# A cross-attention kernel on one core: value and output weights by quads of heads, and other tile shapes

## The chip, the cores and the metric

The kernel runs on one core of a Trainium2 chip. A core has a matrix engine (PE, TensorE), a vector engine (DVE), a scalar engine (ACT), a general engine (POOL, GpSimd), a queue engine (SP) that issues the DMAs here, an on-chip memory of 128 partitions (SBUF), and a matrix-result memory of 8 banks (PSUM), from which ACT and DVE copy results out.

The metric is the device time of one execution in microseconds. Before the change it was 272.81 us (median of three runs, 272.65 to 273.47). The profiled execution took 273.54 us.

## The reference, cut to what matters

Sixteen images of 256 tokens (width 256) attend to sixteen texts of 77 keys (width 192), with 8 heads of 256 each; then an output projection, a residual and a layer norm. All is float32.

```python
Q = (x @ Wq)        # Wq: 256 x (8*256)
K = (c @ Wk)        # Wk: 192 x (8*256)
V = (c @ Wv)        # Wv: 192 x (8*256)
score = einsum('bhqd,bhkd->bhqk', Q, K) / sqrt(256)      # masked by atten_mask
attn = softmax(score)
ctx = einsum('bhqk,bhkd->bqhd', attn, V)
out = ctx @ Wo + x                                       # Wo: (8*256) x 256
return (out - mean) * rsqrt(var + 1e-05) * gamma + beta
```

## The kernel before, in words

The kernel folds weights first. For each head h it forms G_h = Wk_h Wq_h^T (192 x 256) and U_h = Wv_h Wo_h (192 x 256). Scores of an image are then x (G_h^T c^T), and the output is the sum over heads of attn_h (c U_h). The 192 rows of the text width are split in 128 (held in `gA`, `uA`, contracted with `cA`) and 64 (held in `gB`, `uB`, contracted with `cB`); the 64-row parts of two heads or halves lie one above the other.

The order of work is written out by hand (`manual_schedule`): each engine runs its instructions in program order. PSUM tiles come from one pool, `ps_mm`, of 8 buffers, each a bank, all under the tag "mm" and taken in rotation: a new tile waits until the tile eight places earlier has been read out.

Before the main loop over images:

- SP issues all loads in order (lines 620 to 654): whole rows of Wk and Wq for the first head pair (`wk_nat`, `wq_nat`), the first texts, then for pairs a = 1 to 3 blocks `wk_blk` and `wq_blk` (four DMAs each, one for every 32 partitions), `wvT` (16 DMAs, pieces of 512 bytes), `wo_of` (four DMAs of 512 KB), the first images transposed by blocks (`xT`), the mask (`bias`) and the rest of the texts. A load waits for the one eight loads earlier.
- PE begins with `keep_busy(7)`, seven matmuls whose result is not used (L661). The first pair's G is made from transposes on PE (`turn_k`, `turn_q`, `g_of`).
- For pairs a = 1 to 3, DVE turns 32x32 blocks (`turn_blk`, L700), PE makes the 128 rows of G (`g_of_pair`, L798, 64x128 tiles) and the 64 rows (`rest_of_g_of_pair`, L814, 64x64 tiles); ACT copies the one to `gA`, DVE the other to `gB` (four copies, L823). Then `prepare_a` makes A = G^T c^T for the first four images, `part_A` from `gA` (L181, 128x32 tiles) and `part_B` from `gB` (L193, 64x32 tiles). For pair 1 the order is G, rest, A, B; for pairs 2 and 3 both B parts come at the end.
- DVE turns Wv (`turn_v`, L728, four calls, read with a step of 4 floats). PE then makes U: `of_pair` (L738, 64x128 tiles) gives the 128 rows in two halves j of two pairs each, every half in two banks of its own (`pu`); `rest_of_pairs` (L752, 64x64 tiles) gives the 64 rows, again in two halves (`pw`). ACT and DVE copy the results to `uA` (L878) and `uB` (L896). POOL adds up a fifth part of each (`sum_of`, L885 and L886).
- PE makes the scores of the first image (`scores`, L290, four banks). DVE turns the rest of the texts (`turn_rest`, L614 and L616; POOL copies parts of them to `cRA`, `cB`, `cRB`), then reads the score banks (`shift`, L307, 16 calls). ACT makes the exponentials.
- `prepare_last` treats the last 13 keys of all texts at once: eight banks `pr`, each 128 rows by two halves e; `part_A` (L249, 128x64 tiles, two to a bank) and `part_B` (L261, 64x64 tiles) in the order A(0), B(0), B(1), A(1). Four of its eight banks are those that held the scores.

Then the loop over images runs to the end: products with the texts (`pv`, `pa`), scores, softmax, the product with the values by seven block products in place of eight, layer norm, stores.

Of the kernel before, what the change touches and what calls it, by code (L numbers as in the profile page):

```python
# [27 lines left out]
def kernel(  # L28
# [212 lines left out]
    def prepare_last():  # L241


        pr = [ps_mm.tile([P, 2, B, KR], F32, tag="mm", name=f"pr_{n}") for n in range(DI // BK)]

        def part_A(e):
            for n, o in enumerate(pr):
                for i in range(2):
                    nc.tensor.matmul(  # L249
                        o[half(i), e].rearrange("p b k -> p (b k)"),  # L250
                        flat(of_e(uA, e)[:, n])[:, half(i)],
                        flat(cRA),
                        start=(e == 0),
                        stop=(e == 1),
                    )

        def part_B(e):
            for n in range(0, len(pr), 2):
                for i in range(2):
                    for k in range(2):  # L260
                        nc.tensor.matmul(  # L261
                            pr[n + k][half(i), e].rearrange("p b k -> p (b k)"),
                            flat(of_e(uB, e)[half(k), n + k])[:, half(i)],
                            flat(cRB[half(k)]),
                            start=(e == 1),
                            stop=(e == 0),
                        )

        part_A(0)
        part_B(0)  # L270
        part_B(1)
        part_A(1)
        for n, o in enumerate(pr):
            to = vr[:, :, n * BK : n * BK + 2 * KR]
            evacuate(to.rearrange("p b (e k) -> p e b k", e=2), o)
# [303 lines left out]
    with tc.tile_pool(name="wonce", bufs=1) as wp:  # L579
# [52 lines left out]
        wvT = wp.tile([P, NF, NL, P], F32, tag="wvT", name="wvT")  # L632
# [3 lines left out]
        wv_blocks = wv.rearrange("(m r) (a i f) -> a i r m f", r=BK, a=NF, i=NM)  # L636
        wo_rows = wo.rearrange("(a p n) f -> a p n f", p=P, n=4)
        for a in range(NF):
            load_blocks(wvT[:, a], wv_blocks[a])
        for a in range(NF):  # L640
            nc.sync.dma_start(wo_of[a // 2][:, a % 2], wo_rows[a])
# [21 lines left out]
        keep_busy(7)  # L663
# [61 lines left out]
        wv_turned = const.tile([P, NF, 4, DL], F32, tag="vr", name="wv_turned")  # L725

        def turn_v(a):
            nc.vector.transpose(  # L728
                wv_turned[:, a].rearrange("p n (m r) -> p m n r", r=BK),
                wvT[:, a].rearrange("p m (c n) -> p m n c", n=4),  # L730
            )


        def of_pair(out, a, weight, moving):

            for n in range(4):
                for e in range(2):
                    nc.tensor.matmul(  # L738
                        out[e][:, a % 2, :],
                        weight(a, e, n)[:, :P],  # L740
                        moving(a, e, n),
                        start=(n == 0),
                        stop=(n == 3),
                    )

        def rest_of_pairs(j, pairs, weight, moving, name):

            banks = [ps_mm.tile([P, DI], F32, tag="mm", name=f"{name}_{j}_{e}") for e in range(2)]
            for n in range(4):
                for i, a in enumerate(pairs):  # L750
                    for e in range(2):
                        nc.tensor.matmul(  # L752
                            banks[e][half(i)],
                            weight(a, e, n)[:, P:],
                            moving(a, e, n),
                            start=(n == 0),
                            stop=(n == 3),
                        )
            return banks

        def two_banks(name, j):
            return [ps_mm.tile([P, 2, DI], F32, tag="mm", name=f"{name}_{j}_{e}") for e in range(2)]

        def wv_part(a, e, n):
            return wv_turned[half(e), a, n]

        def wo_part(a, e, n):
            return wo_of[a // 2][half(e), a % 2, n, :]
# [24 lines left out]
        def g_of_pair(a):  # L793

            banks = [ps_mm.tile([P, DI], F32, tag="mm", name=f"pgb_{a}_{e}") for e in range(2)]
            for n in range(4):
                for e in range(2):
                    nc.tensor.matmul(  # L798
                        banks[e],
                        kT_blk[a][half(e), n, :P],  # L800
                        qT_blk[a][half(e), n],
                        start=(n == 0),
                        stop=(n == 3),
                    )
# [22 lines left out]
        def a_of_pairs(*pairs):  # L827
            part_A, part_B, copies = prepare_a(0, pairs)
            part_A()
            part_B()  # L830
            for dst, src in copies():
                nc.scalar.copy(dst, src)
# [11 lines left out]
        for a in range(1, NF):  # L844
            g_of_pair(a)
            if a == 2:
                turn_blk(3)
            rest_of_g_of_pair(a)
            if a == 1:
                turn_blk(2)  # L850
                a_of_pairs(1)
            if a == 2:
                second = prepare_a(0, (2,))
                second[0]()
        for i in range(3):
            turn_v(i)
        third = prepare_a(0, (3,))
        third[0]()
        for _, part_B, _ in (second, third):
            part_B()  # L860
        for _, _, copies in (second, third):
            for dst, src in copies():
                nc.scalar.copy(dst, src)
# [4 lines left out]

        for j in range(NF // 2):
            pu = two_banks("pu", j)  # L870
            for a in range(2 * j, 2 * j + 2):
                of_pair(pu, a, wv_part, wo_part)
            if j:
                for i in range(0, GT // 2, 2):
                    transpose_x(0, i)
                bias_of(0, GB)
            for e, copy in enumerate((nc.scalar.copy, nc.scalar.copy if j else nc.vector.tensor_copy)):
                copy(  # L878
                    of_e(uA, e)[:, :, 2 * j : 2 * j + 2].rearrange("p n a c -> p a n c"),
                    pu[e].rearrange("p a (n c) -> p a n c", c=BK),  # L880
                )
# [5 lines left out]

        sum_of(uA)
        for j in range(NF // 2):
            for e, pw in enumerate(  # L890
                rest_of_pairs(j, (2 * j, 2 * j + 1), wv_part, wo_part, "pw")
            ):
                copy = (nc.scalar.copy, nc.vector.tensor_copy)[e]
                for i in range(2):
                    for k in range(2):
                        copy(  # L896
                            of_e(uB, e)[half(k), :, 2 * j + i],
                            pw[half(i)].rearrange("p (n c) -> p n c", c=BK),
                        )
# [191 lines left out]
```

## Time and profile before

| | before |
|---|---|
| median of three runs | 272.81 us (272.65 to 273.47) |
| the profiled execution | 273.54 us |
| its span, first to last instruction | 271.6 us |
| PE busy | 265.3 us, 98% |
| PE weight loads busy | 192.1 us, 71% |
| DVE busy | 185.6 us, 68% |
| POOL busy | 171.4 us, 63% |
| ACT busy | 155.6 us, 57% |
| mean granted PE clock | 0.995 |

A line of a timeline gives the start and the length in us of equal instructions that follow each other, the engine, the line of the kernel, the operation, the tile written and the tiles read, the shape, and how many they are; in brackets stands the idle time before and what ended it. The chain is the work that ended last, followed back from the last instruction: start, length, engine, tile, line. Matmuls overlap, and their ends are modelled, so starts are the firmer numbers. A float32 matmul of the program stands in the trace as two.

### The profile page before, as it was taken

The numbers are of one execution on the slowest core, as the hardware profiler recorded it, in microseconds if no ns is written. First come the engines' busy times: TensorE is split into PE (matmuls) and PEld (weight loads), VectorE is DVE, ScalarE is ACT, GpSimd is POOL, SyncE is SP. The second block draws the span as 40 slices with busy tenths as digits, with TensorE's granted clock in tenths as the row PEclk, the third lists the DMA queues.
The fourth block names the chain that finished last, engine by engine and source line by source line (L and its number), as shares of the span: only waits on it lengthen the run. The fifth ranks groups of instructions, "written<-read, shape, count | busy, mean of one in ns | idle before, by whom it ended". The sixth has DMA issues, their size and how long they took to land.

```text
span 271.6 us, 14367 instructions
## 1 busy us (share of the span) xinstructions
PE 265.3 (98%) x6106; PEld 192.1 (71%) x6106; DVE 185.6 (68%) x809; ACT 155.6 (57%) x652; POOL 171.4 (63%) x231
## 2 busy tenths in 40 slices
PE   8999999999999999999999999999999999999993
PEld 8556588754894499549954996489769969694662
DVE  1455749584366757963795479646977798988765
ACT  3222415834758646873777386739584592945652
POOL 1000005724579766997599759964999798965654
PEclk9999999999999999999999999999999999999998
DMA  6999999998000010271018100910081010110102
GB/s 193 197 197 192 314 164 143 285 151 157 2 5 5 2 42 5 54 146 43 2 37 165 41 6 2 195 42 6 7 190 49 2 45 4 43 41 2 62 22 81
DMA packets 42512, 22.69 MB, mean 84 GB/s; under 512 B 23680, under 2 KB 41680, under 8 KB 42448
## 3 DMA queue, kind: packets, MB, share of 16 engines
q1 hardware_dynamic: 42448, 21.77, 36.8%
q8 instruction: 48, 0.79, 1.3%
q14 instruction: 16, 0.13, 0.2%
HBM read 17.57 MB, written 4.19 MB: 80 GB/s over the span
## 4 chain that ended last, share of the span: by engine, by line
PE 91%; DMA 5%; SPq 2%; DVE 1%; issue 0%; DVEq 0%
PE ps L290 25%; PE pa L181 11%; PE pv L215 10%; PE po L435 10%; PE pm L435 8%; PE pv L226 6%; PE pa L193 5%; DMA wk_blk<-in_L_xattn_Wk_dram 5%; PE po L368 4%; PE pu L738 3%; PE pr L249 2%; PE pgb L798 1%; PE pw L752 1%; PE pr L261 1%; SPq L597 1%; PE po L384 1%
## 5 line engine op out<-in xcount | busy, mean ns | idle before, releaser
L325 ACT ACTIVATE e<-s,top 128x77 f32<-128x77 f32 x256 | 83.8, 346 | 46.6 <-DVE top L307 39.7
L290 PE MATMUL ps<-a,xT 128*32 128x154 f32 x2048 | 69.9, 294 | 0.0
L290 PEld LDWEIGHTS ps<-a,xT 128*32 128x32 f32 x2048 | 66.1, 110 | 1.3 <-ACT uB L896 0.4
L346 POOL TENSOR_TENSOR p<-e,rden 128x512 f32<-128x512 f32 x64 | 47.7, 772 | 24.2 <-DVE rden L340 24.1
L307 DVE CUSTOM_DVE_ANT_0 s<-ps,bias 128x77 f32<-128x77 f32 x256 | 43.5, 232 | 16.3 <-PE ps L290 16.2
L325 ACT ACTIVATION_READ_ACCUMULATOR e<-s,top 128x1 f32 x208 | 38.9, 187 | 0.0
L181 PE MATMUL pa<-cA,gA 128*32 128x308 f32 (+1 forms) x576 | 37.3, 395 | 0.2 <-issue 0.2
L470 POOL TENSOR_TENSOR xg<-xg,m 128x256 f32<-128x256 f32 x39 | 28.7, 737 | 7.8 <-DVE xg L484 5.8
L181 PEld LDWEIGHTS pa<-cA,gA 128*32 128x32 f32 x576 | 18.6, 110 | 20.8 <-issue 8.0
L215 PE MATMUL pv<-uA,cA 128*32 128x512 f32 x256 | 30.6, 595 | 0.0
L553 DVE SCALAR_TENSOR_TENSOR xg<-xg,rstd,bet 128x256 f32<-128x256 f32 x26 | 21.2, 816 | 12.8 <-ACT rstd L514 11.5
L399 POOL TENSOR_TENSOR ts<-vw 128x768 f32<-128x768 f32 x13 | 24.0, 1847 | 8.8 <-ACT vw L933 8.8
L356 DVE STREAM_TRANSPOSE pT<-p 128x640 f32<-128x640 f32 x32 | 25.7, 822 | 3.2 <-POOL p L346 3.1
L933 ACT COPY vw<-pv 128x512 f32<-128x512 f32 x32 | 17.7, 584 | 15.6 <-PE pv L226 7.9
L484 DVE TENSOR_TENSOR xg<-po,xg 128x256 f32<-128x256 f32 x31 | 11.6, 407 | 13.4 <-PE po L435 12.4
L573 POOL TENSOR_TENSOR nan<-nan 128x4 f32<-128x4 f32 (+1 forms) x2 | 0.4, 208 | 32.1 <-DVE nan L572 32.1
L307 DVE DVE_READ_ACCUMULATOR2_ANT top<- 128x1 f32 x256 | 20.7, 81 | 0.0
L193 PE MATMUL pa<-cB,gB 64*32 64x308 f32 (+1 forms) x576 | 20.3, 392 | 0.0
L933 ACT COPY a<-pa 128x308 f32<-128x308 f32 (+1 forms) x56 | 18.9, 399 | 1.7 <-PE pa L181 0.2
L193 PEld LDWEIGHTS pa<-cB,gB 64*32 64x32 f32 x576 | 10.7, 107 | 12.3 <-issue 7.5
L226 PE MATMUL pv<-uB,cB 64*32 64x512 f32 x256 | 17.3, 597 | 0.0
L534 DVE SCALAR_TENSOR_TENSOR xg<-xg,mv,gam 128x256 f32<-128x256 f32 x27 | 16.7, 619 | 0.1
(120 smaller groups left out, 412.3 us busy)
## 6 DMA issues: line engine op xcount, KB each, us to landing
xT<-in_x_dram SPq DMA_DIRECT2D x32, 128.0 KB, 5.6
xg<-in_x_dram SPq DMA_DIRECT2D x6, 512.0 KB, 4.8
out_dram<-xg SPq DMA_DIRECT2D x11, 256.0 KB, 2.4
wo<-in_L_xattn_Wo_dram SPq DMA_DIRECT2D x4, 512.0 KB, 7.2
wq_blk<-in_L_xattn_Wq_dram SPq DMA_DIRECT2D x12, 128.0 KB, 4.6
wvT<-in_L_xattn_Wv_dram SPq DMA_DIRECT2D x16, 96.0 KB, 3.3
out_dram<-xg SPq DMA_DIRECT2D x10, 128.0 KB, 1.7
wk_blk<-in_L_xattn_Wk_dram SPq DMA_DIRECT2D x12, 96.0 KB, 4.5
```

The costliest lines, as they stand in the source:

```text
L181: nc.tensor.matmul(flat(o[i * BK : (i + 1) * BK]), gA[:, h, cols(dc, i)], flat(cA[:, batches, :]), start=not rest_first and n in opening, ...
L193: nc.tensor.matmul(flat(banks[j + k][i * BK : (i + 1) * BK]), gB[half(k), h // 2, cols(dc, i)], flat(cB[half(k), batches, :]), start=rest_ ...
L215: nc.tensor.matmul(pv[k][i * BK : (i + 1) * BK], cA[:, b, k * BK : (k + 1) * BK], uA[:, parts, :, i], start=not rest_first, stop=rest_first,)
L226: nc.tensor.matmul(pv[k][i * BK : (i + 1) * BK], cB[half(k), b, k * BK : (k + 1) * BK], uB[half(k), parts, :, i], start=rest_first, stop=n ...
L290: nc.tensor.matmul(ps[m // 2][i * BK : (i + 1) * BK, m % 2 * 2 * S2 : (m % 2 + 1) * 2 * S2], xT_of[g][:, j * NM + m, dc], flat(a_of[g][:, ...
L307: nc.vector.tensor_tensor_reduce(s[:, h], ps[a][:, k * S2 : (k + 1) * S2], bias[:, b, :], scale=-1.0, scalar=FAR, op0=ALU.add, op1=ALU.min ...
L325: nc.scalar.activation(e[:, h], s[:, h], AF.Exp, bias=top[:, one], scale=-1.0, accum_out=den[:, one] if t < QT * NS else None,)
L346: nc.gpsimd.tensor_tensor(part, e_mh[:, :, :, keys], rden_mh.unsqueeze(3).to_broadcast(list(part.shape)), ALU.mult,)
L356: nc.vector.transpose(pT_of[t].rearrange("p n m q -> p m n q"), p.rearrange("p m (n k) -> p m n k", k=BK),)
L435: nc.tensor.matmul(out[i * BK : (i + 1) * BK], weight[:, i], moving, start=first and n == 0, stop=final and n == len(terms) - 1,)
L470: nc.gpsimd.tensor_tensor(to, to, what, ALU.add)
L933: nc.scalar.copy(dst, src)
```

## The change

Five edits go together.

1. `keep_busy(6)` instead of 7.
2. G of pairs 1 to 3: `g_of_pair` writes 64x64 tiles instead of 64x128 (twice as many matmuls, each with half the columns). `rest_of_g_of_pair` comes before it, and A is made pair by pair, `part_B` first.
3. Wv is loaded in blocks of 256 columns (8 DMAs with pieces of 1 KB), so that each group of 32 partitions holds one head of a quad; Wo is loaded to match. `turn_v` reads with a step of 8 floats.
4. U: `of_quads` replaces `of_pair` and `rest_of_pairs`. One matmul contracts 32 rows of one head; four heads (a quad) run in four row groups and write four banks. The four banks `pu` are used by both quads, each quad's results copied before the next quad's loop in program order; `pw` is one group over both quads, copied after it.
5. `prepare_last`: 128 weight columns to a matmul instead of twice 64.

```diff
         def part_A(e):
             for n, o in enumerate(pr):
-                for i in range(2):
-                    nc.tensor.matmul(
-                        o[half(i), e].rearrange("p b k -> p (b k)"),
-                        flat(of_e(uA, e)[:, n])[:, half(i)],
-                        flat(cRA),
-                        start=(e == 0),
-                        stop=(e == 1),
-                    )
+                nc.tensor.matmul(
+                    flat_of(o[:, e]),
+                    flat(of_e(uA, e)[:, n]),
+                    flat(cRA),
+                    start=(e == 0),
+                    stop=(e == 1),
+                )
...
             for n in range(0, len(pr), 2):
-                for i in range(2):
-                    for k in range(2):
-                        nc.tensor.matmul(
-                            pr[n + k][half(i), e].rearrange("p b k -> p (b k)"),
-                            flat(of_e(uB, e)[half(k), n + k])[:, half(i)],
...
+                for k in range(2):
+                    nc.tensor.matmul(
+                        flat_of(pr[n + k][:, e]),
+                        flat(of_e(uB, e)[half(k), n + k]),
...
-        wvT = wp.tile([P, NF, NL, P], F32, tag="wvT", name="wvT")
+        NQ, NN = NF // 2, DI // BK
+        wvT = wp.tile([P, NQ, NL, D], F32, tag="wvT", name="wvT")
...
-        for a in range(NF):
-            load_blocks(wvT[:, a], wv_blocks[a])
-        for a in range(NF):
-            nc.sync.dma_start(wo_of[a // 2][:, a % 2], wo_rows[a])
+        wv_blocks = wv.rearrange("(m r) (a i f) -> a i r m f", r=BK, a=NQ, i=NM)
+        wo_rows = wo.rearrange("(a p k n) f -> a k p n f", p=P, k=2, n=4)
+        for q in range(NQ):
+            load_blocks(wvT[:, q], wv_blocks[q])
+        for q in range(NQ):
+            for k in range(2):
+                nc.sync.dma_start(wo_of[q][:, k], wo_rows[q, k])
...
-        keep_busy(7)
+        keep_busy(6)
...
         def turn_v(a):
+            q, part = a // 2, slice(a % 2 * 4, a % 2 * 4 + 4)
             nc.vector.transpose(
-                wv_turned[:, a].rearrange("p n (m r) -> p m n r", r=BK),
-                wvT[:, a].rearrange("p m (c n) -> p m n c", n=4),
+                wv_turned[:, q, part].rearrange("p n (m r) -> p m n r", r=BK),
+                wvT[:, q].rearrange("p m (c n) -> p m n c", n=NN)[:, :, part],
             )
...
-        def of_pair(out, a, weight, moving):
...
-        def rest_of_pairs(j, pairs, weight, moving, name):
...
+        def of_quads(quads, out, weights):
+            for n in range(NN):
+                for q in quads:
+                    for i in range(NM):
+                        rows = slice(i * BK, (i + 1) * BK)
                         nc.tensor.matmul(
+                            out(q, i),
+                            wv_turned[rows, q, n, weights],
+                            wo_of[q][rows, n // 4, n % 4, :],
                             start=(n == 0),
+                            stop=(n == NN - 1),
                         )
...
             for n in range(4):
-                for e in range(2):
-                    nc.tensor.matmul(
-                        banks[e],
-                        kT_blk[a][half(e), n, :P],
+                for i in range(2):
+                    for e in range(2):
+                        nc.tensor.matmul(
+                            banks[e][half(i)],
+                            kT_blk[a][half(e), n, half(i)],
...
         for a in range(1, NF):
+            rest_of_g_of_pair(a)
             g_of_pair(a)
-            if a == 2:
-                turn_blk(3)
-            rest_of_g_of_pair(a)
-            if a == 1:
-                turn_blk(2)
-                a_of_pairs(1)
-            if a == 2:
-                second = prepare_a(0, (2,))
-                second[0]()
-        for i in range(3):
-            turn_v(i)
-        third = prepare_a(0, (3,))
-        third[0]()
-        for _, part_B, _ in (second, third):
-            part_B()
-        for _, _, copies in (second, third):
-            for dst, src in copies():
-                nc.scalar.copy(dst, src)
+            if a < NF - 1:
+                turn_blk(a + 1)
+            else:
+                for i in range(3):
+                    turn_v(i)
+            a_of_pairs(a, rest_first=True)
...
-        for j in range(NF // 2):
-            pu = two_banks("pu", j)
-            for a in range(2 * j, 2 * j + 2):
-                of_pair(pu, a, wv_part, wo_part)
-            if j:
...
+        pu = [ps_mm.tile([P, NQ, DI], F32, tag="mm", name=f"pu_{i}") for i in range(NM)]
+        for q in range(NQ):
+            of_quads((q,), lambda q, i: pu[i][:, q], slice(0, P))
+            if q:
+                for i in range(0, GT // 2, 2):
+                    transpose_x(0, i)
+                bias_of(0, GB)
+            for i, o in enumerate(pu):
+                copy = nc.vector.tensor_copy if i % 2 and not q else nc.scalar.copy
+                copy(
+                    of_e(uA, i % 2)[:, :, 2 * q + i // 2],
+                    o[:, q].rearrange("p (n c) -> p n c", c=BK),
+                )
         sum_of(uA)
-        for j in range(NF // 2):
-            for e, pw in enumerate(
-                rest_of_pairs(j, (2 * j, 2 * j + 1), wv_part, wo_part, "pw")
-            ):
-                copy = (nc.scalar.copy, nc.vector.tensor_copy)[e]
...
+        pw = [ps_mm.tile([P, DI], F32, tag="mm", name=f"pw_{i}") for i in range(NM)]
+        of_quads(range(NQ), lambda q, i: pw[i][half(q)], slice(P, DL))
+        for i, o in enumerate(pw):
+            copy = (nc.scalar.copy, nc.vector.tensor_copy)[i % 2]
+            for q in range(NQ):
+                for k in range(2):
+                    copy(
+                        of_e(uB, i % 2)[half(k), :, 2 * q + i // 2],
+                        o[half(q)].rearrange("p (n c) -> p n c", c=BK),
+                    )
```

## The prediction

> **What bounds the kernel now.** I read the page first (busy time, chain), then the chain in order of time, then the timelines of PE, DVE and ACT between 14 and 58 us, where all edits lie, and last the starts of single matmuls there.
>
> ```profile
> span 271.6 us, 14367 instructions
> PE 265.3 (98%) x6106; PEld 192.1 (71%) x6106; DVE 185.6 (68%) x809; ACT 155.6 (57%) x652; POOL 171.4 (63%) x231
> PE 91%; DMA 5%; SPq 2%; DVE 1%; issue 0%; DVEq 0%
> ```
>
> PE works 98% of the span and is 91% of the chain. From 20.57 us to 267 us the chain is matmuls without a break, so what delays or shortens PE's stream after that moves the end by as much; before 20 us the chain is DMA. The stages touched, from the chain (start, length):
>
> ```profile
> 25.82 1.93 PE pgb L798 x16
> 27.74 1.03 PE phb L814 x32
> 28.78 2.21 PE pa L181 x32
> 30.99 2.23 PE pa L193 x64
> 33.22 7.29 PE pu L738 x64
> 40.51 3.62 PE pw L752 x64
> 44.13 4.32 PE ps L290 x128
> 48.45 3.19 PE pr L249 x32
> 51.63 2.98 PE pr L261 x64
> 54.61 2.96 PE pr L249 x32
> 92.19 2.07 PE pa L181 x32
> ```
>
> The reader is to compare equal work: 32 `pa` matmuls take 2.07 us between others of their own shape (last line) and 2.21 after another shape. In the starts of single matmuls all tiles of one shape that fit the array run together, some 7 ns apart, and a round of them takes 216 ns for 256 columns, whether it is one 128x128 tile (`pg`), two 64x128 (`pgb`, `pu`) or four 64x64 (`pw`); 176 ns for 208, 259 for 308, 109 for 128. So tile shape does not change the rate. A change of shape does cost: the first round of the new shape is longer by 24 ns with 32 weight columns, 51 with 64, 104 with 128, and the old shape's last round by 96 to 138.
>
> The two identical halves of `pr` (L249) take 3.19 and 2.96: the first waits. DVE and ACT say for what:
>
> ```profile
> 36.91 0.59 ACT L878 COPY uA<-pu 128x512 f32<-128x512 f32 x1 [2.49 <-PE pu L738]
> 36.95 0.69 DVE L878 COPY uA<-pu 128x512 f32<-128x512 f32 x1 [0.79 <-PE pu L738]
> 42.49 3.49 DVE L896 COPY uB<-pw 64x256 f32<-64x256 f32 x8
> 46.02 1.11 DVE L614 STREAM_TRANSPOSE cA<-cA 128x896 f32<-128x896 f32 x1
> 47.16 1.11 DVE L616 STREAM_TRANSPOSE cB<-cB 64x896 f32<-64x896 f32 x1
> 50.84 0.08 DVE L307 DVE_READ_ACCUMULATOR2_ANT top<- 128x1 f32 x1
> ```
>
> DVE runs without a gap from 40.49 to 50.92: copies of `pw`, two transposes, 16 shifts (2.6 us) that read the score banks. The last four `pr` banks are the score banks; PE waits 0.17 us for the last of them and goes on at 51.06. DVE is thus already the limit at this one place.
>
> **The change, part by part**, in times of this execution (273.54 us; the median of the runs is 272.81, 0.73 less).
>
> *One idle matmul fewer* (L663): 0.43 us of PE (two rounds of 213 ns) before 4 us. It is covered: PE idles later for DMA and DVE.
>
> ```profile
> 14.05 2.00 PE L798 MATMUL pgb<-qT,kT 64*128 64x256 f32 x16 [0.40 <-DVE qT L700]
> ```
>
> Nothing gained; if the clock (rounds of 213 ns until 6.1 us, 109 after) rose up to 1 us later for it, 0.4 of that idle time would cover the most.
>
> *G in 64x64 tiles, rest first.* Same rounds, fewer shapes: `phb` and `pgb` now share one. Before, the stretch from 14.05 to 33.15 has 17.12 us of rounds (24 of 109, 24 of 216, 24 of 259, 12 of 259), so 1.98 of shape changes and one wait of 0.15 at 20.5. After, each pair has `phb`+`pgb`, B, A: 51+110, 24+138, 24+110 ns = 0.46, 1.37 for three. Gain 0.60 (0.3 if only the three first rounds of 104 ns go; 0.9 if the shared ones cost less). New waits: B needs DVE's four `gB` copies (1.25 us), which now run under the 1.73 us of `pgb`; A needs ACT's two copies (0.66), under 1.04 us of B. Both fit. DVE turns the next blocks earlier, by 18.9 for a need at 20.2. `pu` could start at 32.55 instead of 33.15.
>
> *Wv by 256 columns.* SP issues 8 DMAs instead of 16 (some 0.44 us each), then Wo behind them. Wo is nearly late today: its pieces land at 33.01, 34.29, 35.84 and 38.38; the last held `pu` for 0.15 us. Wv lands at 203 GB/s with pieces of 512 B; `wq_nat` with 1 KB at 267, `xg` at 361. I take 267: Wv is in 1.9 us sooner, Wo with it, and the 0.15 goes. Bounds: 1.9 to 3.4 us sooner leave no wait; none sooner and `pu` starts at 33.15, +0.6. The Trainium skill, SBUF — State Buffer, Door 1, speaks against the gain: a DMA into 32 partitions reaches 8 of 16 ports, some 218 GB/s. By it the first piece lands near 32.5, which would add an estimated 0.1 us to the sum.
>
> *turn_v* reads with a step of 8 floats instead of 4. At 4 it takes 1.55 us a call, contiguous (L700, same size) 0.96. I take 1.55, the nearer row: four calls from 28.7 end at 34.9. Up to 1.9 us nothing waits.
>
> *U by quads* (`pu`): 128 matmuls in 32 rounds of four 32x128 tiles, as many rounds as before. 32-row tiles are nowhere in this trace; the bounds are 216 ns (all shapes shown) and 432 (two at a time). I take 216, since three shapes agree. The Trainium skill, TensorE: Matmul & The Clock Gate, Part 3, gives 3.07 times for four row tiles, not 4; by it the 48 rounds of `pu` and `pw` would add an estimated 3.1 us.
>
> *A wait is added in `pu`.* Before, each half has banks of its own. Now the four banks hold both quads, and in the built program the first matmuls of quad 1 wait, bank by bank, for the copies of quad 0: ACT's first, DVE's first, ACT's second, DVE's second. From the last matmul's start to the copy was 0.41 us above; a DVE copy of 128x256 takes 0.42 (L682), a second follows at 0.43; from a DVE end to PE's start 0.14 (50.92 to 51.06). So the fourth bank starts 0.42+0.43+0.42+0.14 = 1.43 us after the last start instead of 0.22, and its second pass reloads weights (0.1): +1.3. Behind it on PE are all the rest. Bounds: 0.7 (only the first bank counts) and 1.7. Quad 1's four copies, all ACT's now (0.37 each), end near 42.9, before the scores need those banks.
>
> `pw` then starts at 32.55+7.14+1.3 = 41.0 and, with 16 rounds as before, ends at 44.61 (before 44.06).
>
> *`pw` in one group.* Before, half of `pw` was complete at 42.25 and DVE copied it while PE did the other half. Now all four banks complete together, so all of DVE's 8 copies (3.5 us) stand behind the end of `pw`. From that end to the last shift it was 6.86 us (44.06 to 50.92); now 0.19+3.50+4.90 = 8.60, +1.74. ACT's 8 copies (2.9) are shorter. PE's scores end at 48.9 and idle behind them; the last `pr` bank starts at 44.61+8.60+0.14 = 53.35, not 51.06: +2.29. Bounds of this step: 1.5 to 1.95. POOL's copies of `cRB` end at about 52.0, earlier.
>
> *Last keys with 128 columns.* The same 48 rounds of 176 ns; three first rounds of 104 instead of 51 ns: +0.17 (0 to 0.3). One thing stays open: at 59.5 us PE stops 0.39 us for no wait shown; with 220 more instructions ahead that may go or appear elsewhere (-0.4 to +0.5). I take 0.
>
> **Sum**: -0.60 -0.15 +1.30 +1.74 +0.17 = +2.46. All later work follows PE, and the rows after 60 us show no wait of PE to absorb it. 273.54+2.46 = 276.0 by this execution, 275.2 by the median.
>
> **Rivals.**
> - *The DVE queue doesn't decide* (copies shorter, or `pr` not held): only -0.60-0.15+1.30+0.17 = +0.7, 273.5, inside 0.3% (0.8 us, about what a measurement of this kernel can tell from no change). Against it: PE already waits there today.
> - *Quads run faster*: if four 32-row tiles cut a round, 48 rounds count. At 168 ns the sum is near nought; below 148 the kernel is faster; at 108, -5.2+2.46 gives 270.1. For it: nothing; three shapes show 216.
> - *Quads run two at a time*: 432 ns, +10.4, 285.6. Against it: two row groups already run together at full rate.
> - *turn_v slows with the wider step*: at 2.5 us a call (the 4-float excess again) the fourth ends at 38.7 and DVE's copies of quad 0 stand behind it: +2.4, 277.6. It decides from 1.9 us on.
> - *The wider Wv pieces bring nothing*: +0.6 at the start of `pu`, 0.15 not saved, 275.9 at most; a part of the forecast's own range.
>
> **How the numbers follow.** Forecast 0.80 (with the last rival), DVE not deciding 0.05, faster quads 0.03, doubled 0.04, slow turn_v 0.08. The forecast's terms at their low ends give -0.9-0.15+0.7+1.5+0-0.4 = +0.75 (273.6), at their high ends -0.3+0.6+1.7+1.95+0.3+0.5 = +4.75 (277.6); all at one end is unlikely, so 273.7 to 277.4 leaves out the faster, the doubled, most of the first rival and some of the slow turn_v: under 2 in 10. Slower: 0.80+0.04+0.08 less 0.02 for the forecast's low tail = 0.90; same 0.07; faster 0.03.
>
> **What would show it.** Right: `pgb` directly behind `phb` with no longer first round; a break of about 1.2 us in `pu` half way, ended by DVE's and ACT's copies of `uA`; `pw` ending near 44.6; DVE's 8 copies starting after it and the first `pr` half ending near 53.9. Wrong: rounds of 32-row tiles unlike 216 ns, turn_v over 1.9 us, a wait for Wo at the start of `pu`, or PE breaks where none stood.

## The result, and the profile after

The changed kernel takes 275.50 us (median of six runs, 275.07 to 276.09), against 273.09 us (272.13 to 273.60) for the kernel before on the same chip: a ratio of 1.0091 with a 95% interval of 1.0067 to 1.0116, so 1.8 to 3.2 us slower. The profiled execution took 275.07 us; that of before took 273.54.

From the page of the changed kernel, the span, the busy time of each engine and the shares of the chain:

```profile
span 273.2 us, 14586 instructions
PE 265.0 (97%) x6216; PEld 192.5 (70%) x6216; DVE 185.9 (68%) x810; ACT 156.8 (57%) x655; POOL 171.4 (63%) x231
PE 80%; DMA 10%; SPq 4%; issue 2%; DVE 1%; POOL 1%; POOLq 0%; DVEq 0%
```

PE's busy time is as before (265.0 against 265.3 us) and the span is 1.6 us longer: PE does the same work and waits more. The chain's share of PE falls from 91% to 80%, because going back from the end it now leaves PE at 49.72 us. The pieces of the chain there (start, length, what):

```profile
44.88 4.40 issue
49.28 0.02 POOLq L618
49.30 0.37 POOL cRA L616
49.67 0.04 issue
49.72 2.15 PE pr L251 x10
```

The 4.40 us of "issue" is a stretch for which the chain found no releaser. The timelines of the engines fill it. First PE, from the end of G on:

```profile
32.52 3.74 PE L744 MATMUL pu<-wo,wv_turned 32*128 32x256 f32 x64
36.70 4.14 PE L744 MATMUL pu<-wo,wv_turned 32*128 32x256 f32 x64 [0.44 <-ACT uA L855]
40.77 3.71 PE L744 MATMUL pw<-wo,wv_turned 32*64 32x256 f32 x128
44.41 4.39 PE L291 MATMUL ps<-a,xT 128*32 128x154 f32 x128
49.72 4.05 PE L251 MATMUL pr<-cRA,uA 128*128 128x208 f32 x16 [0.91 <-POOL cRA L616]
53.70 3.08 PE L262 MATMUL pr<-cRB,uB 64*128 64x208 f32 x32
56.71 3.08 PE L251 MATMUL pr<-cRA,uA 128*128 128x208 f32 x16
```

Two breaks stand where none stood: one in the middle of `pu`, behind the copies of quad 0, and one in front of `pr`. The first half of `pr` is also stretched, 4.05 us against 3.08 for the equal second half. DVE's timeline says what the second break is:

```profile
36.32 0.76 DVE L855 COPY uA<-pu 128x256 f32<-128x256 f32 x2 [1.47 <-PE pu L744]
...
44.61 3.49 DVE L866 COPY uB<-pw 64x256 f32<-64x256 f32 x8 [2.54 <-PE pw L744]
48.13 1.11 DVE L615 STREAM_TRANSPOSE cA<-cA 128x896 f32<-128x896 f32 x1
49.27 1.11 DVE L617 STREAM_TRANSPOSE cB<-cB 64x896 f32<-64x896 f32 x1
```

Before, the eight copies began at 42.49 while PE was still making the other half of `pw`. Now DVE is idle for 2.54 us, begins at 44.61, behind the end of `pw`, and everything in its queue moves back: the turn of `cA` ends at 49.24, POOL then copies `cRA`, and PE starts `pr`. DVE's last shift, which frees the last bank of `pr`, ends at 53.02 instead of 50.91.

The table sets the starts of PE's stages side by side. The last column is what each stage added.

| start of | before | after | later by | added since the row above |
|---|---|---|---|---|
| `pu` | 33.15 | 32.52 | -0.63 | -0.63 |
| `pw` | 40.44 | 40.77 | +0.33 | +0.96 |
| `ps` | 44.06 | 44.41 | +0.35 | +0.02 |
| `pr`, second step | 51.57 | 53.70 | +2.13 | +1.78 |
| `pv`, first of the loop | 57.50 | 59.72 | +2.22 | +0.09 |
| `pv` (64 rows), behind `pa` | 62.35 | 63.65 | +1.30 | -0.92 |

The last row has nothing to do with the two breaks. Before, PE stopped inside the 32 `pa` matmuls that start at 59.24 (the stage took 3.11 us); the changed kernel's profile has no such stop (2.19 us). The lines of before:

```profile
59.24 0.68 PE L181 MATMUL pa<-cA,gA 128*32 128x308 f32 x2
60.15 2.27 PE L181 MATMUL pa<-cA,gA 128*32 128x308 f32 x30 [0.22 <-issue]
```

Some 0.24 us come back near 208 us, where the changed kernel's PE pauses once, 0.20 us. So these two executions are 1.53 us apart, while the medians are 2.41 apart. The profiled execution of before stood 0.73 above its kernel's first median; the stop would explain that, but no other execution of that kernel has a trace.

### The profile page after: what moved, and what is told of

Read it like the earlier page. It is cut to its first block, busy times and chain, and to the rows that moved or that the text cites. A ratio compares the mean times of both kernels' runs of the same rounds, so it can differ in the third digit from the quotient of the medians.

```text
span 273.2 us, 14586 instructions
## 1 busy us (share of the span) xinstructions
PE 265.0 (97%) x6216; PEld 192.5 (70%) x6216; DVE 185.9 (68%) x810; ACT 156.8 (57%) x655; POOL 171.4 (63%) x231
## 4 chain that ended last, share of the span: by engine, by line
PE 80%; DMA 10%; SPq 4%; issue 2%; DVE 1%; POOL 1%; POOLq 0%; DVEq 0%
PE ps L291 23%; PE po L436 10%; PE pv L215 10%; PE pa L181 9%; PE pm L436 8%; PE pv L226 6%; DMA wk_blk<-in_L_xattn_Wk_dram 5%; PE pa L193 5%; PE po L369 4%; DMA xT<-in_x_dram 3%; PE pr L251 3%; DMA wvT<-in_L_xattn_Wv_dram 2%; SPq L145 2%; SPq L598 1%; PE pr L262 1%
## 5 line engine op out<-in xcount | busy, mean ns | idle before, releaser
L181 PE MATMUL pa<-cA,gA 128*32 128x308 f32 (+1 forms) x576 | 36.6, 394 | 0.0
```

Source lines behind the costliest of these rows:

```text
L181: nc.tensor.matmul(flat(o[i * BK : (i + 1) * BK]), gA[:, h, cols(dc, i)], flat(cA[:, batches, :]), start=not rest_first and n in opening, ...
```

## The experiments

In each, the kernel before ran on the same chip; "before" below is that median.

### DVE's queue behind `pw`

The kernel before, but with the copies of `pw` behind both halves, those of the second half first:

```diff
+        ends_of = [
+            rest_of_pairs(j, (2 * j, 2 * j + 1), wv_part, wo_part, "pw") for j in range(NF // 2)
+        ]
         for j in range(NF // 2):
-            for e, pw in enumerate(
-                rest_of_pairs(j, (2 * j, 2 * j + 1), wv_part, wo_part, "pw")
-            ):
+            for e, pw in enumerate(ends_of[1 - j]):
...
-                            of_e(uB, e)[half(k), :, 2 * j + i],
+                            of_e(uB, e)[half(k), :, 2 * (1 - j) + i],
```

> The kernel before, with one thing changed: both halves of `pw` are computed before any of it is copied, the second half's copies first, so that all of DVE's eight copies stand behind the end of `pw`; matmuls, loads and banks stay. Theory (the DVE chain behind `pw` is what delays `pr`): DVE's copies start near 44.2 instead of 42.3, its last shift ends 1.7 to 1.9 later, the last bank of the first half of `pr` starts near 52.8 instead of 51.06, and the time is 1.5 to 1.9 us longer, near 274.6 against 272.9. Rival (the delay of DVE is hidden, and what delayed the changed kernel is the break in `pu` alone): within 0.3 us of the kernel before.

Measured: 274.53 us against 273.30, ratio 1.0049 (1.0023 to 1.0076), so 0.6 to 2.1 us slower, where 1.5 to 1.9 was expected. Its timeline of PE:

```profile
44.37 4.39 PE L290 MATMUL ps<-a,xT 128*32 128x154 f32 x128
49.65 4.04 PE L249 MATMUL pr<-cRA,uA 128*64 128x208 f32 x32 [0.88 <-POOL cRA L615]
53.61 3.04 PE L261 MATMUL pr<-cRB,uB 64*64 64x208 f32 x64
```

The break and the stretched half of `pr` are those of the changed kernel, in a kernel that has none of its tiles, banks or loads. From the start of `ps` to the second step of `pr` it takes 9.24 us, against 7.51 before (44.06 to 51.57): +1.73, and 9.29 in the changed kernel. The theory holds, the rival (hidden) falls.

The same from the other side, the changed kernel with fewer copies on DVE:

```diff
-            copy = (nc.scalar.copy, nc.vector.tensor_copy)[i % 2]
+            copy = nc.vector.tensor_copy if i == NM - 1 else nc.scalar.copy
```

> The changed kernel, but ACT makes 12 of the 16 copies of pw and DVE 4 instead of 8 each. Theory (DVE's queue holds the last pr bank): DVE's shifts end 1.4 to 1.7 us sooner, then limited by the scores; the first half of pr ends near 52.3 instead of 53.7, 1.4 us faster than the changed kernel, about +1.0 against the kernel before. Rival (ACT, whose copies of pw now end near 49.1, delays the exponentials and what hangs on them, or pr isn't held by DVE): under 0.3 us gained.

Measured: 274.49 us against 272.88, ratio 1.0054 (1.0033 to 1.0074). By the medians that is 1.0 us better than the changed kernel's ratio, with intervals that just overlap; 1.4 was expected. In the trace `ps` to the second step of `pr` takes 7.61 us instead of 9.29, so 1.68 came back there, as expected. But 1.08 of it was lost ahead of `pu`, in a place that the edit does not touch:

```profile
29.95 1.22 PE L181 MATMUL pa<-cA,gA 128*32 128x308 f32 x10
31.55 1.76 PE L181 MATMUL pa<-cA,gA 128*32 128x308 f32 x22 [0.38 <-issue]
33.24 3.74 PE L744 MATMUL pu<-wo,wv_turned 32*128 32x256 f32 x64
37.42 4.15 PE L744 MATMUL pu<-wo,wv_turned 32*128 32x256 f32 x64 [0.44 <-ACT uA L855]
41.49 3.71 PE L744 MATMUL pw<-wo,wv_turned 32*64 32x256 f32 x128
```

PE stops at 30.75 and goes on at 31.55, and the profile names no releaser ("issue"). This is taken up below.

### The shared banks of `pu`

The changed kernel, with banks of its own for each quad:

```diff
-        pu = [ps_mm.tile([P, NQ, DI], F32, tag="mm", name=f"pu_{i}") for i in range(NM)]
         for q in range(NQ):
-            of_quads((q,), lambda q, i: pu[i][:, q], slice(0, P))
+            pu = [ps_mm.tile([P, DI], F32, tag="mm", name=f"pu_{q}_{i}") for i in range(NM)]
+            of_quads((q,), lambda q, i: pu[i], slice(0, P))
```

> The changed kernel, but each quad of U has four banks of its own. Theory (the wait of quad 1 for the copies of quad 0 is on the path): no break in pu, pw ends 1.0 to 1.1 us sooner (near 43.35) and so does everything behind it: 1.0 us faster than the changed kernel, +1.3 to +1.4 against the kernel before. Rival (a later wait takes its place, or 32-row tiles are slow by themselves): the end moves by less than 0.3 us, +2.2 or more against the kernel before.

Measured: 274.87 us against 272.88, ratio 1.0079 (1.0054 to 1.0104). The 1.0 us that was expected doesn't show in the times, which don't tell this kernel from the changed one; the trace does. The break is gone, `pw` starts at 39.50 instead of 40.77, and the span is 272.0 instead of 273.2:

```profile
32.23 7.34 PE L744 MATMUL pu<-wo,wv_turned 32*128 32x256 f32 x128
39.50 3.86 PE L744 MATMUL pw<-wo,wv_turned 32*64 32x256 f32 x128
```

Of the 1.27 us, 0.29 is an earlier start of `pu` (a matter of when the first loads land); `pu` itself is 0.98 shorter, 8.25 to 7.27 from start to start. That is the price of the wait inside `pu`. That it reaches the end is seen in this one execution (273.77 us, the lowest of six, against 275.07, the lowest of the changed kernel's).

Both edits together, the changed kernel without its two waits:

> Both: a quad's own banks, and 12 copies of pw on ACT. Theory: the two waits are in series, so the gains add: 2.4 to 2.6 us faster than the changed kernel, -0.2 to 0 against the kernel before (first half of pr ends near 51.2). Rival (one wait hides the other): no better than the better of the two alone, +1.0 against the kernel before.

Measured: 273.77 us (272.56 to 275.91) against 272.88, ratio 1.0036 (1.0012 to 1.0060). Better than the changed kernel by 1.5 us, but not where it was expected: at or under the kernel before. Both waits are gone from the trace. New stops are there; the profiled execution took 275.36 us, 1.6 over the median, so not every execution need have them at this length:

```profile
32.35 6.09 PE L744 MATMUL pu<-wo,wv_turned 32*128 32x256 f32 x104
38.95 1.58 PE L744 MATMUL pu<-wo,wv_turned 32*128 32x256 f32 x24 [0.52 <-issue]
40.46 4.14 PE L744 MATMUL pw<-wo,wv_turned 32*64 32x256 f32 x128
44.52 3.60 PE L291 MATMUL ps<-a,xT 128*32 128x154 f32 x102
48.90 1.21 PE L291 MATMUL ps<-a,xT 128*32 128x154 f32 x26 [0.77 <-issue]
```

The first half of `pr` takes 3.01 us here, so the score banks no longer hold it. But `pu` takes 0.84 us more than the same matmuls without any stop (the experiment after next), `pw` 0.43 more, `ps` 1.18 more (0.95 of it in one stop), and no engine is named for it. Only some 0.16 of what `pu` loses has a cause that the trace shows: the last piece of Wo lands at 37.59, and the round that needs it begins late, at 37.73.

### What stops PE without a name

These stops fit the supply of PE's instructions. The profile's list of DMA queues has one kind that no line of the kernel issues (packets, MB, share of time):

```profile
q8 instruction: 49, 0.80, 1.3%
```

49 packets of 16 KB. PE has 12,432 instructions (6,216 matmuls and as many weight loads), so some 254 a packet, or 127 matmuls, if all packets are PE's. In the DMA records behind this line such a packet ends at 37.44 and at 47.10 us in the execution above, and PE goes on at 38.95 and 48.90, 1.5 and 1.8 us later; in the kernel with ACT's copies a packet ends at 30.28 and PE goes on at 31.55. Counted from the start, the long stops come behind matmul 600 and 854 here and behind 474 in the kernel with ACT's copies: 126 and twice 127 apart. And the stop of the kernel before, at 59.5 us, is behind matmul 852; its packet ended at 58.82, PE went on at 60.15. The kernel with banks of its own, too, is held at matmul 600 and 854, if only by some 0.15 us each; its packets ended at 36.38 and 45.40, PE went on at 37.99 and 46.85. And the pause of the changed kernel near 208 us is behind matmul 4655, 30 times 126.7 behind 854: a packet ended at 206.63, PE went on at 207.90.

Two runs test it. The first is the kernel without the two waits, the same up to `pr`, with `pr` as before the change:

```diff
-                nc.tensor.matmul(
-                    flat_of(o[:, e]),
-                    flat(of_e(uA, e)[:, n]),
...
+                for i in range(2):
+                    nc.tensor.matmul(
+                        o[half(i), e].rearrange("p b k -> p (b k)"),
+                        flat(of_e(uA, e)[:, n])[:, half(i)],
...
```

> The changed kernel without its two waits (banks of their own, ACT with 12 of the copies of `pw`), and with 64 weight columns in `pr` as before the change. Everything ahead of `pr` is the same as in the kernel that only lacks the two waits. Each of the three steps of `pr` then takes 2.96 to 2.98 us instead of 3.01, so the 128 columns cost 0.03 to 0.05 us a step, 0.1 to 0.15 in all, which is less than a time can tell: 273.4 to 273.9. It is a second look at the pauses of PE as well. Theory (they are the arrival of PE's next 16 KB of instructions): they come back at the same matmuls, in round 25 or 26 of `pu`, 12 or 13 of `pw`, 25 or 26 of `ps`, if with other lengths. Rival (disturbances of that one execution): they are gone or elsewhere.

Measured: 273.18 us (271.90 to 277.31) against 272.56, ratio 1.0013 (0.9985 to 1.0041). The profiled execution is the longest of the ten, 277.31 us.

```profile
32.16 6.00 PE L743 MATMUL pu<-wo,wv_turned 32*128 32x256 f32 x104
38.67 1.58 PE L743 MATMUL pu<-wo,wv_turned 32*128 32x256 f32 x24 [0.52 <-issue]
40.18 4.14 PE L743 MATMUL pw<-wo,wv_turned 32*64 32x256 f32 x128
44.24 3.60 PE L290 MATMUL ps<-a,xT 128*32 128x154 f32 x102
48.07 1.21 PE L290 MATMUL ps<-a,xT 128*32 128x154 f32 x26 [0.22 <-issue]
...
55.14 0.57 PE L249 MATMUL pr<-cRA,uA 128*64 128x208 f32 x3
57.86 4.48 PE L249 MATMUL pr<-cRA,uA 128*64 128x208 f32 x29 [2.15 <-issue]
```

The stops are back behind matmul 600 and 854. The second differs in length, and ends 1.50 us behind its packet's end (46.57). A third stands behind matmul 979, 125 further on: from one start to the next it is 2.49 us, and PE goes on 1.54 us behind its packet's end (56.32). Its length is that of this one execution. So the places come back and the lengths do not; the rival (chance) falls for the places. The first two steps of `pr`, ahead of that, take 2.96 and 2.97 us, against 3.01 with 128 columns: 0.04 to 0.05 a step.

The second run takes 48 matmuls away ahead of `pu`: `of_quads` with its own banks and ACT's copies, and G as before the change.

```diff
         for a in range(1, NF):
-            rest_of_g_of_pair(a)
             g_of_pair(a)
...
+            rest_of_g_of_pair(a)
...
```

> The changed kernel without its two waits (the quads of `pu` in banks of their own, ACT with 12 of the 16 copies of `pw`) and with G as before the change: 48 matmuls fewer stand ahead of `pu`. Theory: the pauses of PE without a shown wait that appeared once the two waits were gone (in round 25 of `pu`, round 12 of `pw`, round 25 of `ps`, some 128 matmuls from one to the next) are the arrival of the next 16 KB of PE's instructions, which 128 matmuls with their weight loads use up. With 48 matmuls fewer ahead they move: none in rounds 22 to 28 of `pu`, one if any near round 2 of `pw` and one near round 5 of `ps`. `pu` starts 0.6 to 0.8 us later than in the changed kernel, and the time is 0 to 1.2 us above the kernel before. Rival: the pauses belong to the work (the last piece of Wo, needed in round 24 of `pu`; the score banks): then they stay in round 24 or 25 of `pu` and round 25 of `ps`.

Measured: 273.04 us (272.64 to 273.82) against 273.30, ratio 0.9995 (0.9974 to 1.0015).

```profile
33.20 7.34 PE L744 MATMUL pu<-wo,wv_turned 32*128 32x256 f32 x128
40.47 3.71 PE L744 MATMUL pw<-wo,wv_turned 32*64 32x256 f32 x128
44.11 4.39 PE L291 MATMUL ps<-a,xT 128*32 128x154 f32 x128
```

No stop at all, neither at the old places nor at the new ones that I had named as possible. Here PE comes to matmul 600, 727 and 854 at 2.94, 1.59 and 4.70 us behind the end of the packet, so each was there in time. The other traces agree: in none of the twelve does PE pass matmul 474, 600, 727 or 854 less than 1.27 us behind the end of its packet, and where that packet ended 2 us or more ahead of it no pause of this kind shows. `pu` starts 0.85 us later than with both waits gone and G changed, and yet PE is 1.32 us ahead of that kernel at the first 64-row `pv` (61.68 against 63.00). So 32-row quads without the two waits, with Wo as early as in the change, cost nothing that can be measured against 64-row pairs. In these two executions the stops cost more than the edit of G saves (0.6 us of PE). The times say it less firmly: with G the ratio is 1.0036 (1.0012 to 1.0060), and 1.0013 (0.9985 to 1.0041) with 64 columns, without it 0.9995 (0.9974 to 1.0015), and these intervals overlap. That the packets come late because the loads of the weights and images keep the DMA engines busy until some 64 us is my reading; no run took that load away.

### Where G's gain goes when it stands alone

The kernel before with the edit of G only (the parts of `g_of_pair`, `a_of_pairs` and the loop over pairs in the change's diff; the loop is now):

```python
        for a in range(1, NF):
            rest_of_g_of_pair(a)
            g_of_pair(a)
            if a < NF - 1:
                turn_blk(a + 1)
            else:
                for i in range(3):
                    turn_v(i)
            a_of_pairs(a, rest_first=True)
```

> The kernel before with the edit of G alone (64x64 tiles, rest first, A pair by pair, part_B first); Wv, U, pw and pr as before, seven idle matmuls. Theory: PE's G stage is 0.6 us shorter, so PE could start pu near 32.55, but Wo's first piece lands near 33.0 as before and holds it, and later DVE's queue, whose start is set by the landing of xT near 40.4, holds the last pr bank until 51.06; so less than 0.2 us of the 0.6 reaches the end (272.9 to 273.2 where the kernel before has 273.1). Rival (PE's matmuls alone set the end): 0.6 us faster, 272.5.

Measured: 273.03 us against 272.88, ratio 1.0006 (0.9990 to 1.0022): no difference. In its trace `pu` starts 0.84 us sooner than before, and stands:

```profile
32.31 5.45 PE L738 MATMUL pu<-wo,wv_turned 64*128 64x256 f32 x48
38.73 2.00 PE L738 MATMUL pu<-wo,wv_turned 64*128 64x256 f32 x16 [0.96 <-DMA wo<-in_L_xattn_Wo_dram]
40.65 3.68 PE L752 MATMUL pw<-wo,wv_turned 64*64 64x256 f32 x64
```

The last piece of Wo lands at 38.59, as before the change (38.38), and all that was gained waits for it. The whole change escapes this, since its last piece lands at 36.41 (35.71 to 37.85 in the other kernels with Wv in eight DMAs). Is that the wider piece of Wv (1 KB instead of 512 B) or the smaller number of DMAs? The changed kernel with each load of Wv cut in two:

```diff
-            load_blocks(wvT[:, q], wv_blocks[q])
+            for i in range(NM):
+                for m in (slice(0, NL // 2), slice(NL // 2, NL)):
+                    nc.sync.dma_start(wvT[i * BK : (i + 1) * BK, q, m], wv_blocks[q][i][:, m])
```

> The changed kernel with its eight loads of Wv cut into sixteen: pieces of 1 KB still, 96 KB a DMA. Theory (the number of DMAs ahead in SP's queue sets when Wo is issued): Wv lands at the same rate, some 205 GB/s, but Wo is issued near 27 to 28.5 us instead of 24 to 26.2, and its last piece lands near 38.4 instead of 36.4; `pu` stands some 0.3 us for it in its second half at most. Rival (the 1 KB pieces do it): Wo's last piece lands near 36.4 as in the changed kernel. The time of this one is as the changed kernel's in both cases, within 0.5 us, since the break in `pu` covers the hold.

Measured: 275.22 us, a single run, against 273.30. SP's issues, first of the changed kernel, then of this one (start, length, line, DMAs):

```profile
18.95 5.00 SPq L598 DMA_DIRECT2D wvT<-in_L_xattn_Wv_dram  x8
23.99 2.49 SPq L644 DMA_DIRECT2D wo<-in_L_xattn_Wo_dram  x4
```

```profile
18.01 9.96 SPq L643 DMA_DIRECT2D wvT<-in_L_xattn_Wv_dram  x16
28.01 1.85 SPq L646 DMA_DIRECT2D wo<-in_L_xattn_Wo_dram  x4
```

Wv lands at 208 GB/s (15 loads of 96 KB in 7.10 us) with 1 KB pieces, the first seven of the changed kernel's larger loads at 207, and 202 before with 512 B: the piece size does little, 2 to 3%. Sixteen DMAs take SP 10 us to issue, eight take 5, and Wo follows 4 us later. Its first piece lands no later for it (32.16, against 32.06), its last at 38.48, as in the other kernels with sixteen DMAs ahead of all of Wo (38.38 to 38.70). So it is the number of DMAs that moves the last piece. Eight DMAs with pieces of 512 B were not run.

An order of loads that should bring Wo sooner to the kernel with G alone:

```diff
         for a in range(NF):
             load_blocks(wvT[:, a], wv_blocks[a])
-        for a in range(NF):
-            nc.sync.dma_start(wo_of[a // 2][:, a % 2], wo_rows[a])
+            if a:
+                nc.sync.dma_start(wo_of[(a - 1) // 2][:, (a - 1) % 2], wo_rows[a - 1])
+        nc.sync.dma_start(wo_of[1][:, 1], wo_rows[3])
```

> The kernel before with two edits: G in 64x64 tiles with the rest first, and Wo's first three pieces queued on SP behind the second, third and fourth block of Wv instead of behind all of Wv; U, its tiles, banks and copies stay as before. Theory: the gain of G was lost because `pu` stood for the last piece of Wo, and all DMAs of Wv into 32 partitions ran alone at some 205 GB/s; between them the pieces of Wo, into 128 partitions, use what is left, so the last piece lands 1 us or more sooner (37.4 or before, instead of 38.4 to 38.7), the hold in `pu` shrinks from 1.1 to 0.2 us or nothing, and the time is 0.4 to 0.8 us under the kernel before. Rival (the rate of all loads together is what bounds them, not their order): Wo's last piece lands as before, the hold stays, and the time is within 0.3 us of the kernel before. A loss would come from Wv: its last block is turned at 33.3, and lands later by Wo's share.

Measured: 274.18 us against 272.56, ratio 1.0032 (1.0001 to 1.0064). My theory fell: Wo's last piece comes no sooner, and the kernel is rather slower than faster (the interval only just leaves out 1). PE's timeline:

```profile
36.30 2.00 PE L739 MATMUL pu<-wo,wv_turned 64*128 64x256 f32 x16 [0.55 <-DMA wo<-in_L_xattn_Wo_dram]
39.17 2.00 PE L739 MATMUL pu<-wo,wv_turned 64*128 64x256 f32 x16 [0.87 <-DMA wo<-in_L_xattn_Wo_dram]
41.10 3.68 PE L753 MATMUL pw<-wo,wv_turned 64*64 64x256 f32 x64
```

The last piece lands at 39.03. A load waits for the one eight loads earlier, and SP now stands 1.4 us for a 512 KB piece of Wo in the middle of Wv. The last block of Wv lands at 34.75 instead of 29.9, Wo's third piece at 36.17, and `pu` stands twice.

The same with ACT making all eight copies of the second half of `pw`:

```diff
-                copy = (nc.scalar.copy, nc.vector.tensor_copy)[e]
+                copy = nc.vector.tensor_copy if e and not j else nc.scalar.copy
```

> As the kernel with G in 64x64 tiles and Wo queued between the blocks of Wv, and ACT makes all eight copies of the second half of `pw`, DVE none of them. Theory: once `pu` runs without a hold, DVE's chain behind `pw` is next to set the first half of `pr` (with G alone that half took 3.38 us against 2.96 for the later one); four copies fewer there, 1.74 us of DVE, end it. So the first half of `pr` takes 2.96 to 3.0 us and the time is 0.3 to 0.5 us under the same kernel with DVE's copies. Rival: ACT's copies, 3.0 us behind `pw`, become the next to wait for (they must be done before the second step of `pr`, some 7 us after `pw`): then no gain, or a loss up to 0.5 us.

Measured: 273.32 us against 272.56, ratio 1.0025 (1.0002 to 1.0047). The first half of `pr` takes 2.96 us instead of 3.28, as expected; the 0.3 to 0.5 us that was expected of the time doesn't show (the intervals overlap). None of the ten kernels is faster than the kernel before by more than can be measured.

## Why the prediction was right

Forecast 275.2 us, 2.4 over the kernel before; measured 275.5, 2.41 over it. By its steps:

- *One idle matmul fewer*, taken as nothing: right. The stage of G starts at 14.02, before at 14.05.
- *G*, -0.60: right in size, -0.63 at the start of `pu`, with `pgb` directly behind `phb` as described. My bound for Wo (none sooner, and `pu` starts at 33.15) put that loss at its first piece. With G alone `pu` starts at 32.31 and it is the last piece that takes the 0.60 back.
- *Wv and Wo*, -0.15: right by a wrong step. I took 267 GB/s for 1 KB pieces; it is 207, as before. Wo's last piece comes in 2 us sooner (36.41) because eight DMAs fewer stand ahead of it. The Trainium skill, SBUF — State Buffer, Door 1, which I had weighed against the gain, gives some 218 GB/s as the limit of a DMA into 32 partitions; the 202 to 208 GB/s of the three kernels lie just under it, with either size of the piece.
- *turn_v*, unchanged at 1.55 us a call: right, four calls in 6.06 us (28.79 to 34.85), which ends the rival of a slow turn.
- *Rounds of 216 ns for four 32x128 tiles*: right to the ns (216 in the runs of equal rounds), which ends two rivals (faster, doubled). The Trainium skill, TensorE: Matmul & The Clock Gate, Part 3, gives 3.07 times for four row tiles of 512 columns; here, with 256, the gain is four times, since a round of four takes what one 128x128 tile takes.
- *The wait in `pu`*, +1.30: the mechanism was right, bank by bank in the order described, and the size was off. The fourth bank went on 1.24 us behind the last start of quad 0 (35.89 to 37.13), where I had 1.43, and 0.82 us stands at the break. In all the wait costs 0.98, since `pu` takes 7.27 us without it, in the run with own banks and in the one without G. A term was missing beside it: these 7.27 are 0.13 more than `pu` took before without its 0.15 for Wo (7.14). Without G that stands in the last round (0.48 us against 0.34 before), with own banks at the pause behind matmul 600 (its last round takes 0.32), so whether it is the price of the new shape stays open. Together 0.98 and 0.13, with -0.15 for Wo, make the +0.96 that was measured; I had +1.15.
- *`pw` in one group*, +1.74: right. 9.29 us instead of 7.51 from the start of `ps` to the second step of `pr` is +1.78, of which some 0.04 is the next term; the same order of copies in the kernel before costs +1.73. I had named the shifts as what PE waits for; the copy of `cRA`, behind the same queue, holds the start of `pr` too, and the shifts still set its end.
- *128 columns*, +0.17: 0.09 for the second and third step (3.01 against 2.97 and 2.96), some 0.13 with the first.
- *The stop at 59.5 us*, taken as 0 with bounds of -0.4 to +0.5: in the two profiles it is -0.92, outside the bounds. I had read it as the 0.39 us in which PE is idle; the whole stage was 0.92 longer. It is most of why the profiled execution is at 275.07 and not at 276.0. The median of before, 0.73 under that execution, seems not to contain it, and none of the profiles of the kernels with G alone, with late copies and without the two waits has it; so the sum against the median came out.

At the first `pv` of the loop, ahead of the place of that stop, the terms come to +2.22 where I had +2.46; 0.19 of the difference is the stretch of `pu`. The pause near 208 us, 0.24 us that the sum doesn't have, then brings it back, so that the agreement within 0.3 us is partly luck. And it was reached from the median alone: by the profiled execution of before, with its stop, the same sum gave 276.0 against 275.07.

## What to carry to other kernels

Where two groups of matmuls are merged into one, look at what the copying engine did during the second: its copies now stand behind the whole, and whatever follows in its queue is late by as much, here 1.7 us for a group that PE makes in the same time. Four small tiles in place of two larger ones were free in matmul time here (216 ns a round), but not in instructions nor in the banks that their results occupy, so count both. A saving ahead of a load that is just in time is worth nothing until the load is sooner, and here the number of DMAs in the queue moved it, not their piece size or the one other order that was tried.

## What was unexpected

- PE's own instructions, as I read it, come in packets of 16 KB, one for some 127 matmuls with their weight loads, and a late one stops PE for 0.15 to 2.3 us with nothing named in the profile. PE went on 1.3 to 1.8 us behind the end of the packet in each of the stops above. A stage that uses 128 matmuls in 3.6 us (`pw` in 32x64 tiles) or 4.3 (`ps`), one behind the other, leaves least time for the next packet. In the changed kernel none of this shows in these stages, where PE passes matmul 600, 727 and 854 at 2.06, 2.37 and 1.78 us behind the packet; that the two waits give the packets this time is likely, not shown.
- The last round of `pu` in 32x128 tiles ahead of 32x64 tiles takes 0.48 us in the kernel without stops, that of 64x128 tiles ahead of 64x64 takes 0.34, for a round of 0.216. In the three kernels with `pu` in banks of its own and G changed it takes 0.32, and the last round of `pw` takes 0.50 to 0.54 us there instead of 0.35.
- In the two kernels with G changed and without the two waits the last round of `ps` takes 0.445 us; with G as before it takes 0.245. All of these with odd last rounds have stops near by; the cause stays open.
